# Layer 1's seven products in a ViTDet-like two-layer kernel: w1 in a step of its own, w2 moved between w7 and w4, and the last pair's result one part later

## The chip, the cores and the metric

The kernel runs on one core of a Trainium2 chip, as one program. The metric is device time in microseconds (us). Engines are named as in the profile: PE (TensorE matmul), DVE (VectorE), ACT (ScalarE), POOL (GpSimd) and SP (SyncE, which only issues DMAs here).

## What is computed

Four images of 32 x 32 tokens and 768 channels pass through two residual layers. Each layer is a group norm, an attention with 12 heads of 64 channels and with relative positions by row and column, and an output projection. Layer 1 has in addition a depthwise 3 x 3 convolution and a layer norm on each head's Q, K and V, and adds Q to the attention's result.

```python
x = x + conv0(gn(x))                      # layer 0: plain Q, K, V
x = x + conv1(gn(x))                      # layer 1
# conv1, per image and head:
q, k, v = (layer_norm(dwconv3x3(t, w_pool)) for t in split(x @ w_qkv.T + b_qkv))
attn = q * scale @ k.T + rel_h + rel_w    # rel_* = q with the table of offsets
o = softmax(attn) @ v + q
return o @ w_proj.T + b_proj
```

## The kernel before

**Stages, pairs and items.** A stage is one image's pass through one layer. The order of the eight is (image, layer) = (0,0), (1,0), (0,1), (1,1), (2,0), (3,0), (2,1), (3,1). A stage is six pairs of heads; hp = 0 to 5 is a pair's index in its stage. The 48 pairs are numbered through, and the attention of pair n is called item n here. An item has 16 steps: for each half c of the 512-column query blocks, twice (scores for four key blocks in two steps, product with V in two steps). Layer 1 is in items 12 to 23 and 36 to 47.

**Pieces.** Everything else is cut into pieces hung on steps. `plan` (L833 to L900) lists the pieces of pair i with a step r that counts from the start of item i-1; a negative r lies in item i-2. So during item n the pieces of pair n+1 (r = 0 to 15) and of pair n+2 (r = -16 to -1) run. PE, DVE, ACT, POOL and SP each take their instructions in the order in which the program lists them; an instruction that waits holds all behind it on its engine.

**Seven products.** For a pair of layer 1 whose two predecessors are also in layer 1 (`in_products`, 20 pairs: 14 to 23 and 38 to 47) Q and K of both halves of the tokens, a product of 2 x 2 blocks (token half by channel half, channel half by Q or K), are made by seven products, w1 to w7, instead of eight, with weights (`mix_weights`) and token blocks (`sum_tokens`, the sums S1 to S4) added up in advance. Each product is 12 matmuls. `products(n)` issues them:

- w1, w2 and w6 come first. In 14 of the pairs (hp not 1 or 4) they are at step -7, w1 and w6 summed in one bank; w7 follows at -6 and w4 at -5 in the same bank. In the six early pairs (hp 1 and 4) w1, w6 and w2 are at -8, and w7 and w4, each in a bank of its own, at -6 with two DVE adds (L666, L669).
- w5 at step -4 and w3 at step -2 follow in both; add(w3) (L681) at step 0. `put_from` (L593) is the ACT copy from PSUM to the padded tile.
- DVE then runs the convolution's taps (L706), the layer norm (L721 to L744), ACT the exponentials.

**Other pieces near.** `positions(g)` (L775) is the relative position run on PE, 128 small matmuls a group, two groups a pair, followed by two ACT copies (L780, L781). `split` (L791, L792) splits its result. `back` (L753) transposes the normalised Q and K on PE (tile ln_t). `call` (L605) loads the three token blocks of a sum on SP's queue. `sum_tokens` writes these sums through tile x; `mix_weights` adds up weight sets with five DVE subtractions or additions.

**The result of a pair.** The last row of the pair's attention result is the sum for the softmax. It is turned around by `invert` (a reciprocal on DVE, L950, which waits for a DMA of that row), restored by `restore_last` (PE, L989, tile last) and multiplied by `weighed_result`. These are parts, taken one after another behind scores and products of the next item (L1121 to L1133). The pair with hp = 5 has a list of parts of its own.

Of the kernel before, what the change touches and what calls it, by code (L numbers as in the profile page):

```python
# [17 lines left out]
P = 128  # L18
# [33 lines left out]
def two_layers(ctx: ExitStack, tc: tile.TileContext, keep, x_in, wqkv, wproj, rels, windows, vrow, small, const, onehot, picks, out):  # L52
# [79 lines left out]
    def small_bank(name):  # L132
        return ps_small.tile([P, 512], F32, tag="small", name=name)
# [84 lines left out]
    def in_products(i):  # L218

        return all(items[k][1] == 1 for k in (i, i - 1, i - 2))  # L220

    def shift(i):

        return 4 if i and items[i][1] == 0 and items[i - 1][1] == 1 else 0
# [64 lines left out]
    def used(use):  # L289
        load_weights(uses.index(use) + 2)  # L290
# [53 lines left out]
    def sum_tokens(stage):  # L344


        for n in range(NC // 2):
            x11, x12, x21, x22 = (xns[stage][:, n + k, h : h + HALF] for h in (0, HALF) for k in (0, 3))

            def keep_sum(which, x, y, op):  # L350
                to = wp.tile([P, HALF], F32, tag="x", name="token_sum")
                nc.vector.tensor_tensor(to, x, y, op)
                nc.sync.dma_start(tokens[stages.index(stage) % 2][which, n], to)
                return to

            s1 = keep_sum(S1, x21, x22, ALU.add)
            s2 = keep_sum(S2, s1, x11, ALU.subtract)
            yield
            keep_sum(S4, x12, s2, ALU.subtract)
            yield  # L360
            keep_sum(S3, x11, x21, ALU.subtract)
            yield

    def group_norm(stage):
# [69 lines left out]
    class Pair:  # L434
# [175 lines left out]
            for n in range(3):  # L610
                halves(ps, w[:, n, :], x[n], start=not (n or more), stop=n == 2, skip_group_check=True)

        def second(self):

            self.seven(self.w12, 2, [xns[self.b, self.layer][:, 3 + n, :HALF] for n in range(3)], more=True)
            self.put_from(0, 0, self.w12)

        def products(self, n):

            Q, K = 0, 1
            xn = xns[self.b, self.layer]
            x = {(h, k): [xn[:, 3 * k + n, h * HALF : (h + 1) * HALF] for n in range(3)] for h in range(2) for k in range(2)}
            add = lambda to, x, y: nc.vector.tensor_tensor(to, x, y, ALU.add)  # L627
            early = self.hp in (1, NC // 2 + 1)
            if n == 0:
                temps = one.tile([P, 2, HALF], F32, tag="k0", name="temps")  # L630
                self.u, self.x = temps[:, 0], temps[:, 1]
                self.pad[Q] = in_turn("pad", pads)
                if not early:
                    self.sum, w2 = bank("sum"), bank("w2")
                    self.seven(self.sum, 0, x[0, 0])
                    nc.scalar.copy(self.x, self.sum)
                    self.seven(w2, 2, [xn[:, 3 + m, :HALF] for m in range(3)])
                    self.seven(self.sum, 1, self.blocks, more=True)
                    used((self.i, 0, 0))
                    self.call(S3)  # L640
                    add(w2, w2, self.x)
                    self.put_from(Q, 0, w2)
                    nc.scalar.copy(self.u, self.sum)
                    return
                self.w12, w6 = bank("w1w2"), bank("w6")
                self.seven(self.w12, 0, x[0, 0])
                nc.scalar.copy(self.u, self.w12)
                self.seven(w6, 1, self.blocks)
                used((self.i, 0, 0))
                self.call(S3)  # L650
                self.second()
                add(self.u, self.u, w6)
            elif n == 1 and not early:
                self.seven(self.sum, 3, self.blocks, more=True)
                used((self.i, 0, 1))
                self.call(S1)
                nc.scalar.copy(self.x, self.sum)
            elif n == 5:
                self.seven(self.sum, 4, x[1, 1], more=True)
                self.put_from(Q, 1, self.sum)  # L660
            elif n == 1:
                w7 = bank("w7")
                self.seven(w7, 3, self.blocks)
                used((self.i, 0, 1))
                self.call(S1)
                add(self.x, self.u, w7)  # L666
                w4 = bank("w4", place_b)
                self.seven(w4, 4, x[1, 1])
                add(w4, w4, self.x)  # L669
                self.put_from(Q, 1, w4)  # L670
            elif n == 2:
                self.pad[K] = in_turn("pad", pads)
                w5 = small_bank("w5")
                self.seven(w5, 5, self.blocks)
                used((self.i, 0, 2))
                self.call(S4)
                add(self.u, self.u, w5)
                add(w5, w5, self.x)
                self.put_from(K, 1, w5)
            elif n == 4:  # L680
                add(self.w3, self.w3, self.u)  # L681
                self.put_from(K, 0, self.w3)
            else:
                self.w3 = bank("w3")
                self.seven(self.w3, 6, self.blocks)
                used((self.i, 0, 3))
                after = self.i + 1
                if after < len(items) and in_products(after) and items[after][2]:
                    pairs[after].call(S2)
# [57 lines left out]

        def back(self, s, h):

            ps = bank("ln_t")  # L750
            for t in range(NKT // 2):
                g = h * (NKT // 2) + t
                nc.tensor.transpose(ps[:, t * P : (t + 1) * P], self.c[s][:, g * P : (g + 1) * P], ident)  # L753
            g = LN + 2 * s
            if s == 0:
                self.put_q(ps, h, col(g), col(g + 1))
            else:
                self.put_k(ps, h, sk[:, g : g + 1], sk[:, g + 1 : g + 2])

        def positions(self, g):  # L760


            if g == 0:
                self.whole = one.tile([P, T], F32, tag="whole", name="whole")
            ps = bank("rel")
            for k in range(S // 2):
                at = g * (S // 2) + k
                for j in range(2):
# [36 lines left out]
        def plan(self):  # L805
# [31 lines left out]
            late = self.hp in (0, NC // 2)  # L837
            early_late = self.hp in (1, NC // 2 + 1)
            if in_products(self.i):
                steps = (-8 if early_late else -7, -6, -4, -2, 0)  # L840
                pieces = [(r, lambda n=n: self.products(n)) for n, r in enumerate(steps)]
                if self.hp not in (1, NC // 2 + 1):
                    pieces.append((-5, lambda: self.products(5)))
                if not (self.hp and in_products(self.i - 1)):
                    pieces.insert(0, (-10, lambda: self.call(S2)))
            else:
                pieces = [
                    (-8 if early_late else -7, lambda: self.padded(Q, 0)),
                    (-6, lambda: self.padded(Q, 1)),
                    (-4, lambda: self.padded(K, 0)),  # L850
                    (-2, lambda: self.padded(K, 1)),
                ]
            between = self.i + 1 < len(items) and in_products(self.i + 1) and self.hp + 1 not in (1, NC // 2 + 1)
            positions_1 = lambda: self.positions(1)
            positions_1.last = between
            pieces += [
# [8 lines left out]
                (9, lambda: self.back(Q, 1)),  # L865
                (10, lambda: self.square(K)),
                (11, lambda: self.squares(K)),
                (11 if between else 10, lambda: self.positions(0)),
                (11, positions_1),
                (12, lambda: self.norm(K)),  # L870
                (11 if short(self.i) and self.hp == NC - 1 else 12, lambda: self.split()),
# [39 lines left out]
    def attend(pair, os):  # L911
# [20 lines left out]
        for c in range(T // QC):  # L932
# [152 lines left out]
            for g in range(0, NKT, 4):  # L1085
# [35 lines left out]
                if g + 4 == NKT:  # L1121

                    if not pair.layer:
                        parts = (sums, result, finish) if last(c) else (sums, spread, call, spread_finish)
                    elif not by_ones[c]:
                        parts = (landed, sums, result)
                    elif (pair.hp, c) == (NC - 1, 1):
                        parts = (invert, only_restore, weighed_result)
                    elif short(pair.i) and (pair.hp, c) in ((NC - 2, 1), (NC - 1, 0)):
                        parts = (landed, invert, only_restore, weighed_result)  # L1130
                    else:
                        parts = (landed, invert_and_restore, landed, weighed_result)
                    rest.extend(parts)  # L1133
                    found = copy(av)
# [136 lines left out]
    for k in range(1, len(stages)):  # L1271
# [3 lines left out]
        if stages[k][1]:  # L1275
            places = (34, 37, 41, 41, 50, 50, 53, 55, 57, 59, 61) if stages[k - 1][1] else range(27, 60, 3)
            token_sums = sum_tokens(stages[k])
            for r in (60, *range(64, 72)) if stages[k - 1][1] else range(58, 67):
                at(first + r, lambda token_sums=token_sums: next(token_sums))
        else:  # L1280
            places = (34, 37, 41, 41, 50, 50, 53, 55, 58, 61, 64) if stages[k - 1][1] else range(34, 67, 3)
# [13 lines left out]
    for u, call, step in (  # L1295
        (2, 0, 5), (7, 6, 11), (3, 13, 18), (4, 22, 29), (8, 31, 38), (5, 40, 47), (0, 49, 55), (6, 57, 63), (1, 65, 71),
        (9, 72, 77), (10, 78, 83), (11, 84, 89), (17, 114, 119), (18, 120, 125), (19, 126, 131), (20, 132, 137),
        (15, 212, 217), (14, 226, 233), (16, 258, 265), (12, 266, 274), (13, 275, 281),
    ):
        mix = mix_weights(u)  # L1300
        for at_step in (call, step):
# [361 lines left out]
```

## Time and profile before

| what | value |
|---|---|
| median of 3 runs (lowest to highest) | 3785.4 us (3783.3 to 3787.0) |
| the profiled execution | 3783.47 us |
| its span | 3781.5 us |
| PE busy | 3688.4 us, 98% |
| DVE busy | 2463.0 us, 65% |
| ACT busy | 1724.8 us, 46% |
| POOL busy | 617.4 us, 16% |
| mean granted clock of PE | 0.998 |

The busy shares are averages over the span; the profile's slices show DVE at six to eight tenths in layer 1 and fewer in layer 0. The time of a wait is the idle time of an engine before an instruction, with the event that ended it.

### The profile page before, as it was taken

The page shows a single profiled execution, that of the slowest core. Times are in us where ns is not written, and L with a number is a line of the kernel's source. Part 1 is how long each engine was busy: PE and PEld are TensorE (multiplying, and loading weights), DVE is VectorE, ACT ScalarE, POOL GpSimd, SP SyncE. Part 2 cuts the span into 40 slices and gives each one's busy share as a digit, 9 for nine tenths or more (in the row PEclk, how much of TensorE's full clock was granted, in tenths as well). Part 3 has the DMA queues.
Part 4 walks back from the last instruction along what each step waited for, and adds up shares of the span by engine and source line. Part 5 has one row for each costly group of instructions (what it writes and reads, how often), then busy time and mean ns, then how long its engine had stood idle before and what let it go on. Part 6 is the DMA issues. An engine that isn't in the chain of part 4 may idle for free.

```text
span 3781.5 us, 77865 instructions
## 1 busy us (share of the span) xinstructions
PE 3688.4 (98%) x32926; PEld 1640.7 (43%) x32926; DVE 2463.0 (65%) x3181; ACT 1724.8 (46%) x2438; POOL 617.4 (16%) x1152
## 2 busy tenths in 40 slices
PE   8999999999999999999999999999999999999998
PEld 4535535534344433444535445355343444334442
DVE  2566555559678877688454554445686788767884
ACT  2455434545345553455434544244452555434551
POOL 0111100110121221022310010001101122212130
PEclk9999999999999999999999999999999999999999
DMA  4444454431543564442344232523225435354333
GB/s 149 115 133 125 143 147 130 118 102 49 163 151 106 157 172 117 144 128 81 81 119 132 62 89 69 172 69 107 82 55 167 133 101 165 89 152 118 86 92 103
DMA packets 267347, 441.87 MB, mean 117 GB/s; under 512 B 43446, under 2 KB 115538, under 8 KB 266992
## 3 DMA queue, kind: packets, MB, share of 16 engines
q1 hardware_dynamic: 189008, 321.60, 27.1%
q0 software_dynamic: 77984, 115.21, 13.1%
q8 instruction: 263, 4.31, 0.5%
q14 instruction: 92, 0.75, 0.1%
HBM read 275.38 MB, written 60.39 MB: 89 GB/s over the span
## 4 chain that ended last, share of the span: by engine, by line
PE 82%; DVE 10%; issue 3%; DMA 3%; ACT 1%; POOL 1%; SPq 0%; DVEq 0%; ACTq 0%; POOLq 0%
PE s L1091 15%; PE av L1115 14%; PE qkv L138 9%; PE m1m L138 5%; PE m3m L138 4%; PE m4m L138 4%; PE sum L138 4%; PE s L1093 4%; PE w L138 4%; PE p3p L138 3%; PE p1p L138 3%; PE rel L775 3%; DVE shared L706 2%; PE p4p L138 2%; PE m L138 2%
## 5 line engine op out<-in xcount | busy, mean ns | idle before, releaser
L1098 ACT ACTIVATE e<-s 128x1024 f32<-128x1024 f32 x768 | 767.3, 1023 | 357.7 <-PE s L1093 332.8
L1091 PE MATMUL s<-q,k 64*128 64x512 f32 x3072 | 811.2, 604 | 13.1 <-ACT e L1098 4.7
L706 DVE SCALAR_TENSOR_TENSOR shared<-shared,sm 128x1056 f32<-128x1056 f32 x576 | 757.5, 1315 | 14.9
L1093 PE MATMUL s<-bias,ones 64*128 64x512 f32 x1536 | 613.8, 790 | 0.9 <-DMA bias<-high 0.9
L1115 PE MATMUL av<-e,vt 128*64 128x512 f32 x2624 | 595.9, 596 | 0.1
L802 POOL DMA_DIRECT2D bias<-high x384 | 202.0, 546 | 1774.9 <-ACT high L791 1494.6
L1109 DVE TENSOR_TENSOR acc<-acc,e 128x1024 f32<-128x1024 f32 x294 | 360.2, 1225 | 117.1 <-ACT e L1098 90.9
L1091 PEld LDWEIGHTS s<-q,k 64*128 64x128 f32 x3072 | 279.7, 186 | 276.2 <-issue 195.0
L138 PE MATMUL qkv<-xn,wqkv_t 128*64 128x512 f32 x1728 | 387.3, 598 | 0.9 <-DVE xn L408 0.9
L1115 PEld LDWEIGHTS av<-e,vt 128*64 128x64 f32 x2624 | 184.8, 137 | 347.3 <-issue 300.5
L1093 PEld LDWEIGHTS s<-bias,ones 64*128 64x128 f32 x1536 | 149.8, 187 | 182.9 <-issue 176.2
L138 PEld LDWEIGHTS qkv<-xn,wqkv_t 128*64 128x64 f32 x1728 | 121.1, 138 | 236.5 <-issue 230.7
L802 POOL DMA_DIRECT2D bias<-whole x384 | 206.2, 566 | 43.5 <-DVE whole L792 30.9
L593 ACT ACTIVATE shared<-qkv,sm 128x512 f32<-128x512 f32 (+1 forms) x128 | 57.4, 502 | 284.2 <-PE qkv L138 284.2
L938 ACT COPY weighed<-av 128x512 f32<-128x512 f32 x96 | 56.3, 586 | 246.5 <-PE av L1115 237.3
L1107 DVE TENSOR_TENSOR acc<-e 128x1024 f32<-128x1024 f32 x49 | 60.0, 1224 | 164.0 <-PE z L1013 116.2
L775 PEld LDWEIGHTS rel<-q,rel 64*32 64x32 f32 x6144 | 112.8, 106 | 74.6 <-issue 60.0
L593 ACT ACTIVATE shared<-w,sm 128x512 f32<-128x512 f32 x120 | 53.8, 503 | 196.4 <-DVE w L627 196.4
L956 POOL DMA_DIRECT2D inv<-z_inv x94 | 51.5, 552 | 516.6 <-DVE z_inv L950 428.6
L775 PE MATMUL rel<-q,rel 64*32 64x32 f32 x6144 | 124.3, 195 | 8.5 <-issue 8.5
L721 DVE TENSOR_REDUCE mean<-ln_c 128x8 f32<-128x512 f32 x144 | 98.6, 685 | 48.3 <-PE ln_c L718 48.3
L775 PE MATMUL rel<-q_t,rel 64*32 64x32 f32 x6144 | 125.2, 195 | 4.4 <-issue 4.4
(208 smaller groups left out, 5057.1 us busy)
## 6 DMA issues: line engine op xcount, KB each, us to landing
bias<-high POOLq DMA_DIRECT2D x384, 128.0 KB, 3.3
bias<-whole POOLq DMA_DIRECT2D x384, 128.0 KB, 4.2
blocks<-tokens SPq DMA_DIRECT2D x160, 256.0 KB
wqkv_t<-mixed SPq DMA_DIRECT2D x86, 384.0 KB
wqkv_t<-in_wqkv SPq DMA_DIRECT2D x126, 192.0 KB
third_block<-tokens SPq DMA_DIRECT2D x80, 256.0 KB
wproj_t<-mixed SPq DMA_DIRECT2D x48, 384.0 KB
wqkv_t<-in_wqkv SPq DMA_DIRECT2D x38, 384.0 KB
```

The lines of the kernel that those rows point to most:

```text
L138: nc.tensor.matmul(ps[lo : lo + D], a[:, lo : lo + D], b, start=start, stop=stop, **kw)
L593: nc.scalar.activation(self.pad[s][:, rows, there : there + src.shape[2]], src, AF.Identity, bias=col(self.column(s)))
L706: nc.vector.scalar_tensor_tensor(y, window, tap, y, ALU.mult, ALU.add)
L721: nc.vector.tensor_reduce(of, heads, AX.X, ALU.add)
L775: nc.tensor.matmul(ps[lo : lo + S, k * S : (k + 1) * S].rearrange("p (b c) -> p b c", b=2), rel[rows, 2 * self.layer + i, first : first + ...
L802: nc.gpsimd.dma_start(sets, some.unsqueeze(1).to_broadcast([D // 2, 2, QC]))
L1091: nc.tensor.matmul(ps[:, j, :], k[rows, keys], q[rows, cols], start=True, stop=False)
L1093: nc.tensor.matmul(ps[:, j, :], ones[rows, kt % 2 * P : (kt % 2 + 1) * P], bias[c][rows, kt // 2, :], start=False, stop=True,)
L1098: nc.scalar.activation(e, ps, AF.Exp)
L1107: nc.vector.tensor_tensor(acc, es[0], es[1], ALU.add)
L1109: nc.vector.tensor_tensor(acc, acc, e, ALU.add)
L1115: nc.tensor.matmul(av[j * D : (j + 1) * D, :], pair.vt[:, kt, j * D : (j + 1) * D], e[:, j, :], start=(kt == 0), stop=(kt == NKT - 1),)
```

## The change

In 16 of the 20 pairs (all but hp 2; `in_chain`) w1 stands alone at step -8 with an ACT copy into tile high, w6 is at -7, w7 and w2 are at -6 with one DVE add, and w4 at -5. The first position run of the pair before moves to step 10, ahead of w7 and w2; the second stays at 11. The hp 2 pairs (14, 20, 38, 44) take the form that the early pairs had, with w1, w6 at -7 and w2, w7, w4 at -6. For pairs 17 and 41 (hp 5, with another layer-1 stage behind) the reciprocal and the result come one part later. The token sums S3 are issued last, over the last three calls, and five weight mixes are issued at other steps.

```diff
+    def in_chain(i):
+        return i < len(items) and in_products(i) and items[i][2] != 2
...
-            keep_sum(S3, x11, x21, ALU.subtract)
+        for n in range(NC // 2):
+            xn = xns[stage]
+            to = wp.tile([P, HALF], F32, tag="x", name="token_sum")
+            nc.vector.tensor_tensor(to, xn[:, n, :HALF], xn[:, n, HALF:], ALU.subtract)
+            nc.sync.dma_start(tokens[stages.index(stage) % 2][S3, n], to)
             yield
...
+            if n == 0 and in_chain(self.i):
+                self.w1 = one.tile([P, T], F32R, tag="high", name="w1")[:, :HALF].bitcast(F32)
+                self.sum = bank("sum")
+                self.seven(self.sum, 0, x[0, 0])
+                nc.scalar.copy(self.w1, self.sum)
+            elif n == 6:
+                self.seven(self.sum, 1, self.blocks, more=True)
+                used((self.i, 0, 0))
+                self.call(S3)
+                nc.scalar.copy(self.u, self.sum)
+            elif n == 1 and in_chain(self.i):
+                self.seven(self.sum, 3, self.blocks, more=True)
+                self.call(S1)
+                nc.scalar.copy(self.x, self.sum)
+                w2 = bank("w2", place_b)
+                self.seven(w2, 2, x[0, 1])
+                used((self.i, 0, 1))
+                add(w2, w2, self.w1)
+                self.put_from(Q, 0, w2)
...
-            ps = bank("ln_t")
+            ps = small_bank("ln_t") if s == 0 and h and in_chain(self.i + 1) else bank("ln_t")
...
-            ps = bank("rel")
+            between = in_chain(self.i + 1) and self.layer
+            ps = small_bank("rel") if between and g else bank("rel", place_b) if between else bank("rel")
...
-                steps = (-8 if early_late else -7, -6, -4, -2, 0)
+                steps = (-8, -6, -4, -2, 0, -5, -7) if in_chain(self.i) else (-7, -6, -4, -2, 0)
...
-                    pieces.insert(0, (-10, lambda: self.call(S2)))
+                    pieces.insert(0, (-8, lambda: self.call(S2)))
...
-                (11 if between else 10, lambda: self.positions(0)),
+                (10, lambda: self.positions(0)),
...
-                    elif (pair.hp, c) == (NC - 1, 1):
+                    elif (pair.hp, c) == (NC - 1, 1) and short(pair.i):
                         parts = (invert, only_restore, weighed_result)
                     elif short(pair.i) and (pair.hp, c) in ((NC - 2, 1), (NC - 1, 0)):
                         parts = (landed, invert, only_restore, weighed_result)
                     else:
                         parts = (landed, invert_and_restore, landed, weighed_result)
...
-            for r in (60, *range(64, 72)) if stages[k - 1][1] else range(58, 67):
+            for r in (60, 64, 67, 68, 70, 71, 72, 72, 73) if stages[k - 1][1] else range(62, 71):
...
-        (15, 212, 217), (14, 226, 233), (16, 258, 265), (12, 266, 274), (13, 275, 281),
+        (15, 138, 147), (16, 149, 159), (12, 220, 228), (13, 268, 276), (14, 277, 283),
```

## The prediction

> **What bounds the kernel now.** First the page: the profiled execution took 3783.47 us, 1.97 us of it outside the span, and lies 1.9 us below the median of the runs (3785.4).
>
> ```profile
> span 3781.5 us, 77865 instructions
> PE 3688.4 (98%) x32926; PEld 1640.7 (43%) x32926; DVE 2463.0 (65%) x3181; ACT 1724.8 (46%) x2438; POOL 617.4 (16%) x1152
> ```
>
> PE sets the end: it is idle for 93 us in all. PE's list of instructions keeps its count in this change (the seven products stay seven), so a gain can come only from those 93 us, from time at a lower clock, and from new idle time on the other side. Hence the second view, the waits of PE: us in total, times, longest.
>
> ```profile
> PE rel L775 <- issue: 12.9, 10, 2.2
> PE w L138 <- ACT shared L593: 11.0, 6, 2.2
> PE last L989 <- ACT shared L593: 9.7, 2, 5.0
> PE s L1091 <- ACT e L1098: 4.7, 6, 1.0
> PE sum L138 <- PE ln_t L753: 3.4, 14, 0.2
> PE m3m L138 <- DVE shared L475: 2.7, 3, 1.3
> PE s L1091 <- DVE shared L722: 2.2, 3, 0.8
> PE s L1091 <- ACT whole L781: 1.6, 4, 0.4
> PE sum L138 <- DMA blocks<-tokens: 1.5, 2, 0.8
> ```
>
> The change touches each of these lines. "Item n" is below the attention of pair n, which runs beside pieces for pairs n+1 and n+2. I placed every gap above 0.4 us in its item. Third view: VectorE's timeline in item 20, one of the six items that prepare an index-1 or index-4 pair.
>
> ```profile
> 1668.61 0.70 DVE L627 TENSOR_TENSOR w<-w,temps 128x512 f32<-128x512 f32 x1 [1.95 <-PE w L138]
> 1669.22 1.21 DVE L732 TENSOR_REDUCE lnv<-shared 128x16 f32<-128x1024 f32 x1
> ...
> 1670.55 2.67 DVE L706 SCALAR_TENSOR_TENSOR shared<-shared,sm 128x1056 f32<-128x1056 f32 x2
> 1673.13 0.77 DVE L704 TENSOR_SCALAR shared<-shared,sm 128x1056 f32<-128x1056 f32 x1
> 1673.93 5.45 DVE L706 SCALAR_TENSOR_TENSOR shared<-shared,sm 128x1056 f32<-128x1056 f32 x4
> ...
> 1683.00 0.69 DVE L627 TENSOR_TENSOR w<-w,temps 128x512 f32<-128x512 f32 x1
> ```
>
> Read it as one chain: DVE waits for the product w4, then squares, seven taps, norm, split, and only then the two adds that free w5 for the copies of L593; from the first add's start to those copies' end (1684.69) it is 16.07 us. PE needs only 14.14 us from the end of w4 (1668.51) to the end of the work ahead of product w3 (1682.64), so it stands 2.09 us. The same view in item 18:
>
> ```profile
> 1418.10 0.34 DVE L950 RECIPROCAL z_inv<-z_inv 32x32 f32<-32x32 f32 x1 [6.67 <-DMA z_inv<-z]
> ```
>
> A reciprocal at the head of DVE's queue waits 6.67 us for its DMA, the add of w3 stands behind it, and PE's `last` stands 5.05 us; item 42 is the same with 4.66.
>
> Fourth, the granted clock in windows from the end of a gap (PE busy, instructions, clock, DMA):
>
> ```profile
> 1243.51:1244.51 1.00, 1.00 (x6) 0.50 0.07 16
> 1684.73:1685.73 1.00, 1.00 (x6) 1.00 1.06 221
> ```
>
> After gaps of 2.17, 2.20, 4.66 and 5.05 us the clock is at half for 3.41 us, which loses 1.71 us; after gaps of 2.09 and 2.10 us it stays full.
>
> [...]
>
> **Part 1, w2 behind w7 (16 pairs).** w1 stands alone a step earlier, then ln_t, w6, and after the first position run w7, w2, w4. PE's work is the same. ACT gains four 0.58 us copies, DVE loses four 0.68 us adds; ACT is 46% busy, so nothing. w6 now waits for the copy of w1 out of the same bank; ln_t (1.09 us) covers the copy (0.58 us after 0.1 us); without that cover it costs 0.7 us per pair. ln_t comes forward by two products in the six items: in item 20 its source is ready 36.15 us into the item, w1 ends at 36.40, so it just fits.
>
> - *w3.* DVE's chain now starts at w2, which ends one product (2.68 us with its change-over) earlier against w3: PE has 16.82 us, DVE and ACT need 16.07 plus 0.13 of signalling, margin 0.6. The five stalls of items 14, 20, 38, 41, 44 (2.17+2.09+2.10+2.09+2.10 = 10.55) go, and the half clock behind item 14's 2.17: **12.3**. The other ten pairs, which had no such stall, now have the same margin.
> - *rel.* The two position runs, 128 matmuls each, lie 2.65 us apart in ten items, and in eight of them PE stalls in the middle of the second (2.20, 1.38, 0.49, 1.40, 0.25, 1.41, 0.91, 1.44 = 9.48). Where runs lie at least 3.5 us apart, in 37 other items, there is no stall. They come to lie three products (7.7 us) apart. With the half clock after 2.20: **11.2**. Items 22 and 46 (1.83, 1.61; back to back) are untouched.
> - *Small ones.* The 0.24 us of sum behind ln_t in ten of fourteen places, less 0.4 for changed neighbours: 2.0. s behind `whole` (4 x 0.41): 1.6, as the second run no longer ends the step. **3.6**.
> - *New.* The add to w2 waits for PE and holds the rest of DVE's queue. In items 15 and 39 two normalisations of xn (1.45) and a pair of token sums (1.32) stand between it and w5's adds: 2.77 - 0.6 = 2.15 each, 4.3; that is at the edge between 2.10 and 2.17, so half of 2 x 1.71 is added: **6.0** (bounds 4.3 and 7.7). Item 17: 2.59 for a mix less 0.6 is 2.0, against 1.8 before: 0.2.
>
> **Part 2, the last pair's reciprocal one part later (items 18, 42).** The chain of its DMAs lands while DVE goes on to the add of w3, and `last` is reached some 1.5 us after the copies it waits for. The two waits go (5.05+4.66 = 9.71) with two half clocks (3.42): **13.1**. If the result is then late for its own reader, the next part still lies a whole score-and-product step behind, so I take nothing.
>
> **Part 3, token sums and weight mixes.** The S3 sums come last, some later than before, by one to two steps. Waits of sum for blocks (0.80+0.72) go, since the load is issued earlier: 1.5. s behind L722 in 16 and 40 (0.69+0.72): 1.4, as fewer sums stand ahead of it; 1.4 of the e waits there likewise; 0.6 in item 34. **4.9**. Against it: the third S3 block is written two steps before w7 reads it; in 16 and 40 write plus load (2.1 to 4.6 and 3.1 to 5.1 us in the trace) leaves 0 to 3 us each; I take 0.5, near the short end, as queue neighbours there are short: 1.0. SP's order changes: mixes' loads go ahead of some weight loads and S1 and S2 loads change places with them; no weight load is in the list of waits, so nothing. POOL keeps its list. Item 10 gets a mix's subtractions and sums ahead of the add that m3m waits for (1.29 now): one more us carries it over 2.17, so 1.0+1.71 = 2.7 (bounds 1 and 5).
>
> **Sum.** 12.3+11.2+3.6+13.1+4.9 = 45.1 back; 6.0+0.2+1.0+2.7 = 9.9 lost; net 35.2. 3783.47 - 35.2 = 3748.3; on the scale of the median 1.9 more: 3750.
>
> **Rivals.** *Slower: w3 stalls in all 16 pairs.* For: DVE is 81 to 94% busy in these items, its chain of taps stands behind an add that PE's late product releases, and the margin is 0.6 us where ten pairs had several. Against: in item 20 DVE stood idle 1.95 us before that add, and two adds ahead of it are gone. Once DVE reaches the add 0.6 us late every further us is PE's, times 16; at 2.2 us each the gain is eaten (35), and just there the half clock sets in with 1.71 more: 16 x 3.9 = 62, net +27, 3812. So it decides at 2.8 us of lateness, and just under it there is no change.
>
> *The rel stall is not tied to distance.* The profile names no releaser for it ("issue"), so that it is instructions running out is my reading of where it falls; then 11.2 stays: 3761.4, say 3761. For it: at the same 2.65 us item 37 stalls for 0.25 only and item 13 not at all; against it: none in 37 items with the runs further apart.
>
> [...]
>
> *The moved sums collide.* All bounds at once: 7.7 in 15 and 39, 5 in item 10, 3+1.71 in 16 and 40 each (9.4): 22 instead of 9.7 lost: 3763.
>
> **How the numbers follow.** Forecast (3741 to 3757) 0.55; rel 0.13; collisions 0.14; w3 everywhere 0.12; more gained than I count 0.06. The range 3740 to 3770 takes in the first three and leaves out 0.15 or so. About 0.2%, 7.6 us, is what a measurement can tell from no change: all but the w3 rival are faster by more, 0.88; of its 0.12, 0.03 is no change and 0.09 slower.
>
> **What would show it.** In the profile after: no wait of w for L593 above 0.7 us outside items 15, 17 and 39; `last` gone from the list of waits; rel left with the two of items 22 and 46 (3.4); half clock only where a gap passes 2.1 us. PE busy stays near 3680, idle falls from 93 to some 60. A row "w <- ACT shared" with 10 or more entries would make the prediction wrong, and so would rel stalls at 7.7 us distance.

## The result, and the profile after

The changed kernel takes 3750.0 us (median; 3748.99 to 3754.77) against 3784.35 us for the kernel before in the same comparison. The ratio is 0.9911 with a 95% interval of 0.9894 to 0.9928: faster by 0.9%, or 34 us. The profiled execution of the changed kernel was the slowest of its four, 3754.77 us, 4.8 us above the median; against the profiled execution of before it is 28.7 us shorter.

The page of the changed kernel, span and busy time:

```profile
span 3753.0 us, 77916 instructions
PE 3688.4 (98%) x32926; PEld 1628.6 (43%) x32926; DVE 2457.9 (65%) x3177; ACT 1725.3 (46%) x2442; POOL 617.7 (16%) x1152
```

PE has as many matmuls and the same busy time as before to the tenth of a us. The gain is idle time: span less busy time is 64.6 us, where it was 93.1. The waits of PE (us in total, times, longest), the rows that answer to those of before:

```profile
PE w L138 <- ACT shared L601: 6.5, 3, 2.2
PE s L1096 <- ACT e L1103: 4.5, 6, 1.2
PE rel L782 <- issue: 4.1, 2, 2.2
PE m3m L138 <- DVE shared L483: 3.5, 3, 2.2
PE w L138 <- DMA third_block<-tokens: 2.4, 2, 1.2
```

`last` is gone from this list, and so are sum behind the blocks and s behind `whole`; of sum behind ln_t (3.4 in 14 places) 1.0 in four is left, now before w1. The wait of w for L601 (L593 before) fell from 11.0 to 6.5, that of rel from 12.9 to 4.1, and what is left of rel is items 22 and 46, which the change does not touch (3.4 before). m3m went up, and the wait for the third block is new.

How the time of each item moved tells more than the totals. (Item n starts with the first score product of pair n; us, changed kernel less kernel before, from the two profiled executions.)

| items | change | what it is |
|---|---|---|
| 14, 20, 38, 41, 44 | -4.09, -2.16, -2.18, -2.10, -2.17 | the wait at w3; in 14 also its half clock |
| 18, 42 | -7.37, -7.02 | `last` behind the reciprocal, with its half clock |
| 13, 19, 21, 37, 43 | -1.50, -0.73, -1.47, -0.47, -1.90 | rel (in 13 the wait for the blocks), and the small waits |
| 16, 40 | -3.67, -2.56 | rel, and what stood behind the token sums |
| 15, 39 | +1.38, +3.91 | rel gone (in 15 with its half clock), new waits at w3 and half clock |
| 9, 10, 34 | +1.48, +2.61, -1.43 | m3m behind the moved sums and mixes, in 10 with half clock |
| 22, 46, 47 | +1.15, +0.45, +2.01 | the untouched rel stall, in 22 a wait for ACT, in 47 a half clock |

The chain on VectorE in item 20, which stood in the prediction, now looks like this (start, us, engine, line, operation; in brackets the idle time before it):

```profile
1653.62 0.70 DVE L630 TENSOR_TENSOR w<-w,w 128x512 f32<-128x512 f32 x1 [0.78 <-PE w L138]
1654.22 1.21 DVE L738 TENSOR_REDUCE lnv<-shared 128x16 f32<-128x1024 f32 x1
...
1658.93 5.45 DVE L712 SCALAR_TENSOR_TENSOR shared<-shared,sm 128x1056 f32<-128x1056 f32 x4
...
1668.01 0.69 DVE L630 TENSOR_TENSOR w<-w,temps 128x512 f32<-128x512 f32 x1
```

From the first add's start to the end of the last it is 15.08 us, as before (1668.61 to 1683.69). What moved is PE: w2 is now followed by w4, so PE comes to w3 a product later, and the copies end 0.52 us before the work ahead of w3 does. In 13 of the 16 pairs this room is 0.51 to 0.53 us, and in the other three (items 15, 17 and 39) it is used up.

### The profile page after: what moved, and what is told of

It is laid out like the page before. It is cut to its first block, busy times and chain, and to the rows that moved or that the text cites. A ratio compares the mean times of both kernels' runs of the same rounds, so it can differ in the third digit from the quotient of the medians.

```text
span 3753.0 us, 77916 instructions
## 1 busy us (share of the span) xinstructions
PE 3688.4 (98%) x32926; PEld 1628.6 (43%) x32926; DVE 2457.9 (65%) x3177; ACT 1725.3 (46%) x2442; POOL 617.7 (16%) x1152
## 3 DMA queue, kind: packets, MB, share of 16 engines
q8 instruction: 263, 4.31, 0.5%
## 4 chain that ended last, share of the span: by engine, by line
PE 88%; DVE 6%; DMA 2%; ACT 2%; issue 2%; POOL 0%; SPq 0%; DVEq 0%; ACTq 0%; POOLq 0%
PE av L1120 16%; PE s L1096 16%; PE qkv L138 9%; PE m1m L138 5%; PE sum L138 5%; PE m3m L138 4%; PE m4m L138 4%; PE w L138 4%; PE s L1098 4%; PE p3p L138 3%; PE rel L782 3%; PE p1p L138 3%; PE p4p L138 2%; PE m L138 2%; PE ln_c L724 2%
## 5 line engine op out<-in xcount | busy, mean ns | idle before, releaser
L601 ACT ACTIVATE shared<-qkv,sm 128x512 f32<-128x512 f32 (+1 forms) x128 | 57.5, 503 | 281.8 <-PE qkv L138 281.8
L601 ACT ACTIVATE shared<-w,sm 128x512 f32<-128x512 f32 x120 | 53.7, 503 | 160.7 <-DVE w L630 160.7
L138 PE MATMUL m3m<-xn,wqkv_t 128*64 128x512 f32 x528 | 122.6, 600 | 3.5 <-DVE shared L483 3.5
```

The lines of the kernel that those rows point to most:

```text
L138: nc.tensor.matmul(ps[lo : lo + D], a[:, lo : lo + D], b, start=start, stop=stop, **kw)
L601: nc.scalar.activation(self.pad[s][:, rows, there : there + src.shape[2]], src, AF.Identity, bias=col(self.column(s)))
```

## The experiments

**The reciprocal alone, from both sides.** First the changed kernel without it:

```diff
-                    elif (pair.hp, c) == (NC - 1, 1) and short(pair.i):
+                    elif (pair.hp, c) == (NC - 1, 1):
                         parts = (invert, only_restore, weighed_result)
```

> The changed kernel with the last pair's reciprocal and result where they were before. Theory, that the reciprocal at the head of DVE's queue holds the add of w3 and so PE's tile last: 5.05 + 4.66 of waits and two half clocks of 1.71 come back, 13.1 more, about 3763. Rival, that the rearranged adds of the seven products have taken that wait away by themselves: no change against 3750.

Measured: 3762.97 us, ratio 0.9943 (0.9930 to 0.9957), 13.0 us above the changed kernel. Its list of waits has `last` again, somewhat shorter than in the kernel before (8.3 for two), and each of the two comes with half clock. Then the same line the other way round, in the kernel before:

> The kernel before with one edit: the last pair's reciprocal and result one part later. Theory: the two waits of last (9.7) and their two half clocks (3.4) go, 13.1 less, about 3771, and nothing else moves. Rival, that the later result is late for its own readers: as much comes back at the head of items 18 and 42, 3784.

Measured: 3769.72 us, ratio 0.9967 (0.9955 to 0.9979), 12.5 us below the kernel before in this comparison (3782.18). Items 18 and 42 are 6.9 and 6.5 us shorter in its trace, and no wait of `last` is in its list. The two runs agree: this one line is worth 12.5 to 13 us of the 34, with either order of the products.

**The distance between the position runs.** In the kernel before, only this was changed:

```diff
-                (11 if between else 10, lambda: self.positions(0)),
+                (10, lambda: self.positions(0)),
```

> The kernel before with one edit: the first position run one step earlier, ahead of w7, so that the two runs lie two products (5.2 us) apart and not one (2.65 us) in the items that had one product between. Theory, that the stall goes with distance: 9.5 of stalls and one half clock of 1.7 go, 11 less, about 3773. Rival, that the stall has another cause: the rel waits stay at 9 to 13 us and the time at 3784.

Measured: 3787.25 us, ratio 1.0012 (1.0003 to 1.0021), no gain and, if anything, slower by 0.1%. Its waits of PE show why theory and rival both fell short:

```profile
PE sum L138 <- ACT temps L657: 10.4, 14, 0.7
...
PE rel L775 <- issue: 4.4, 2, 2.4
```

The stall did go with the distance: the runs now lie 6.2 us apart in nine of the ten items and 7.2 in one, none of the ten has it any more, and the two places left are items 22 and 46. But a new wait took its place in 14 items. w4 adds to the bank in which w7 has just ended, and ACT has to copy that bank first (L657). In the kernel before, the position run lay between the two products and hid this copy; with the run moved ahead of w7, nothing hides it:

```profile
1237.49 0.59 ACT L657 COPY temps<-sum 128x512 f32<-128x512 f32 x1 [1.16 <-PE sum L138]
1238.13 1.08 PE L138 MATMUL sum<-xn,wqkv_t 128*64 128x512 f32 x4 [0.74 <-ACT temps L657]
```

So 9.5 us of stall were traded for 10.4 us of waits; two waits for the third block (3.2 us in items 15 and 39) are new as well. In the change it is w2 that fills this place.

**w2 on the other side of w7.** That gives the next experiment, in the changed kernel:

```diff
-                self.seven(self.sum, 3, self.blocks, more=True)
...
                 w2 = bank("w2", place_b)
                 self.seven(w2, 2, x[0, 1])
+                self.seven(self.sum, 3, self.blocks, more=True)
...
```

> The changed kernel with w2 ahead of w7 in the 16 pairs, so that w4 stands right behind w7 again. Theory, that w2 between w7 and w4 is what hides ACT's copy of their common bank (0.74 us of wait in each of 14 items in before_runs_apart): 16 x 0.74 = 12 come back, and w2 itself has to wait for the two copies out of the first run's bank if it shares that bank (1.6 us less 0.5, 16 x 1.1 = 18); against it w3 has a product more of room, which takes away its three waits (6.5) and the half clocks behind them: 3756 to 3774. Rival, that the order of the two makes no difference to PE: 3743 to 3750, from w3's room alone.

Measured: 3758.0 us, ratio 0.9935 (0.9918 to 0.9952), 8 us above the changed kernel. The copy's wait is there in all 16 pairs:

```profile
PE sum L138 <- ACT temps L652: 11.0, 16, 0.7
```

The row of w behind L601 is gone, as expected: in this order the room before w3 is 1.45 to 1.52 us in 14 of the pairs and 0.47 in items 15 and 39. In these two w3 waits for the third block all the same (1.76 and 2.26 us): that wait comes even where VectorE's chain does not hold up w3. Wrong in the expectation was the other term: no wait of w2 for the copies of the first position run is in the trace, since it gets another bank. So w2 between w7 and w4 gives up 1 us of room at w3 and saves 0.69 us of waiting in each pair, a good trade where the room is not used up.

**The runs together.** The opposite of the change, for the stall alone:

```diff
-                (11, positions_1),
+                (10, lambda: self.positions(1)),
```

> The changed kernel with the second position run right behind the first, ahead of w7 and w2. Theory, that the stall goes with the distance between the two runs: each of the 20 items stalls as items 22 and 46 do (1.98 and 2.17 in the changed kernel's profile), some 40 us; w2 ends one run (1.3) later, which is 0.8 over the 0.5 of room before w3, some 13 more; half clocks on top where a gap passes 2.1: 3800 to 3820. Rival, that distance has nothing to do with it: no rel waits but the two there are, only the 13 at w3, about 3763.

Measured: 3831.98 us, ratio 1.0133 (1.0117 to 1.0148), 82 us above the changed kernel and more than expected:

```profile
PE rel L782 <- issue: 44.6, 21, 2.7
PE w L138 <- ACT shared L601: 16.8, 16, 2.2
```

The stall comes back in 17 of the 20 items at 1.8 to 2.7 us each (not in 18, with 0.1 in 16, and in 21 only behind the run, 1.8 us inside the product that follows), and in two others at the edge of the stages; it falls anywhere between the 24th and the 125th matmul of the second run. The expectation's 40 + 13 us of waits are there; too low was its price for the clock: 17 stretches of half clock and one at the end, at a granted clock of 0.992. Half of the time at half clock, the most that it can cost, is 31.2 us, where it is 12.7 in the changed kernel.

**The room before w3.** Four more adds of 128x512 behind the add to w2:

```diff
                 add(w2, w2, self.w1)
+                for _ in range(4):
+                    add(self.w1, self.w1, self.w1)
```

> The changed kernel with four more adds of 128x512 (2.7 us) on DVE right behind the add to w2 in each of the 16 pairs. Theory, that the room before w3 is 0.5 us (from the profile: the copies end 0.51 to 0.53 before the work ahead of w3 does) and every us beyond is PE's: 2.2 us in 13 pairs and 2.7 in the three that have none left, 37 us, and a half clock of 1.7 in some of them, 3787 to 3814: the gain is gone or more. Rival, that DVE catches the time up in its idle stretches: within 5 of 3750.

Measured: 3804.34 us, ratio 1.0059 (1.0044 to 1.0075): slower than the kernel before. The waits of PE, two rows:

```profile
PE w L138 <- ACT shared L601: 33.9, 16, 2.2
...
PE ln_t L761 <- DVE shared L752: 12.6, 16, 3.0
```

The delay shows at two places, since the transposes ahead of w3 wait for the same chain; at w3 itself it is 2.17 or 2.18 us in 15 of the 16 pairs and 1.30 in item 15. Half of the time at half clock is 29.8 us, at a granted clock of 0.992. This is the prediction's slower rival made real: 2.7 us of work at this place turn a gain of 34 us into a loss of 22.

**Token sums and mixes as before.** The third part of the change undone (order and steps of `sum_tokens`, steps of the five mixes):

```diff
-            for r in (60, 64, 67, 68, 70, 71, 72, 72, 73) if stages[k - 1][1] else range(62, 71):
+            for r in (60, *range(64, 72)) if stages[k - 1][1] else range(58, 67):
...
-        (15, 138, 147), (16, 149, 159), (12, 220, 228), (13, 268, 276), (14, 277, 283),
+        (15, 212, 217), (14, 226, 233), (16, 258, 265), (12, 266, 274), (13, 275, 281),
```

> The changed kernel with the token sums and the weight mixes of the kernel before (order and steps). By the prediction's sum this part is worth 4.9 back less 3.7 lost: 1 us, so about 3751: the waits of items 9 and 10 shrink by 1.5 and 2.6, items 15 to 17 and 40 get more sums and mixes ahead of what PE waits for. Rival, that the moved work is what makes room for the new order of the products: new waits at w3 or s in items 14 to 17 and 39 to 41 of 2 us each, 3760 and more.

Measured: 3750.92 us, ratio 0.9920 (0.9906 to 0.9933), not to be told from the changed kernel. In the trace items 9, 10 and 17 are 1.5, 2.1 and 2.1 us shorter than in the changed kernel, items 14, 16 and 34 are 1.2, 1.5 and 1.6 us longer. This part moves waits about and is worth nothing as a whole.

**What stands behind the add to w2 in items 15 and 39.** The changed kernel's waits there are new. PE in item 15:

```profile
1253.91 2.61 PE L138 MATMUL w<-blocks,wqkv_t 128*64 128x512 f32 x8 [2.18 <-ACT shared L601]
1257.71 1.97 PE L138 MATMUL w<-third_block,wqkv_t 128*64 128x512 f32 x4 [1.19 <-DMA third_block<-tokens]
```

VectorE, and SP's own queue, in the same item:

```profile
1235.01 0.70 DVE L630 TENSOR_TENSOR w<-w,w 128x512 f32<-128x512 f32 x1 [4.96 <-PE w L138]
1235.62 1.52 DVE L416 TENSOR_SCALAR xn<-xn,gmean,r_gn 128x1024 f32<-128x1024 f32 x2
...
1247.85 0.69 DVE L356 TENSOR_TENSOR token_sum<-token_sum,xn 128x512 f32<-128x512 f32 x1
```

```profile
1234.93 0.33 SPq L276 DMA_DIRECT2D wqkv_t<-in_wqkv  x1
1247.85 1.05 SPq L357 DMA_DIRECT2D tokens<-token_sum  x2
1249.00 1.82 SPq L613 DMA_DIRECT2D blocks<-tokens  x2
1250.88 0.48 SPq L271 DMA_DIRECT2D wqkv_t<-in_wqkv  x1
1251.41 0.51 SPq L613 DMA_DIRECT2D third_block<-tokens  x1
```

DVE waits 4.96 us for w2, and only behind that add come the normalisation and the sums that were ready to run in this time. The sum's write waits for DVE at the head of SP's queue, and the blocks that w3 needs are loaded behind it. So they were moved to the other side of the add:

```diff
-            places = (34, 37, 41, 41, 50, 50, 53, 55, 57, 59, 61) if ...
+            places = (34, 37, 41, 41, 50, 50, 53, 55, 57, 57, 61) if ...
...
-            for r in (60, 64, 67, 68, 70, 71, 72, 72, 73) if ...
+            for r in (58, 64, 67, 68, 70, 71, 72, 72, 73) if ...
```

> The changed kernel with two normalisations of xn two steps earlier and the first token sum two steps earlier, so that they stand ahead of the add to w2 on DVE and not behind it (items 15 and 39; DVE waits there 4.96 us before that add). Theory, that DVE work behind this add is what delays w3 and that a sum's write holds the next blocks' load on SP's queue: the w3 waits of 2.18 and 2.18, the third-block waits of 1.19 and 1.22 and both half-clock stretches of 6.83 us go, 6.8 + 6.8 = 13.6 less, about 3736. Rival, that VectorE is simply full there: the waits come back elsewhere in items 15, 16, 39, 40 and the time stays within 3 of 3750.

Measured: 3744.07 us, ratio 0.9895 (0.9879 to 0.9910), 5.9 us less than the changed kernel's median, though the two intervals overlap. In the trace items 15 and 39 are 5.4 and 5.8 us shorter and neither wait is left in them; DVE's wait ahead of the add fell from 4.96 to 2.18 us. Items 16 and 40 took 0.6 and 0.7 us back. The time is 8 us above the 3736 expected. The expectation took half of each 6.83 us at half clock as lost, but PE stood idle for 1.2 us of it, which costs nothing more. It also counted the half clock of one profiled execution as if it were in every run; the granted clock of the changed kernel is 0.997 in that execution and 0.998 in its other three.

**A faster version.** With that edit, the last mix one step earlier, and layer 0's mixes and sums in other steps:

> As norm_and_sum_ahead, and besides: the last mix one step earlier (ahead of the add to w2 in item 17), two mixes of layer 0 in other steps of item 9 with their loads behind the result's row on SP's queue, and the layer-0 token sums kept out of the first steps of items 10 and 34. Theory: the w3 wait of item 17 (2.1, at times with a half clock) goes, and the m3m waits of items 9 and 10 (1.1 to 2.0 and 2.2 with a half clock) shrink by 3 to 5: 5 to 8 below norm_and_sum_ahead, about 3738. Rival: SP's queue or the two buffers of tile x make them come back elsewhere, 3744.

Measured: 3739.86 us, ratio 0.9891 (0.9876 to 0.9906). Item 17 is 2.2 us shorter than in the changed kernel, item 9 by 1.4. PE still waits 2.6 us in item 10: a mix and two token sums share the two buffers of tile x and waited for each other's writes. Once more, with these apart (against the changed kernel; the edit of norm_and_sum_ahead is in it too):

```diff
-        (15, 138, 147), (16, 149, 159), (12, 220, 228), (13, 268, 276), (14, 277, 283),
+        (15, 146, 150), (16, 151, 154), (12, 220, 228), (13, 268, 276), (14, 277, 282),
...
-  else range(62, 71):
+  else (60, 61, 62, 66, 67, 68, 69, 70, 71):
```

> As ahead_and_mixes_moved, with the two mixes of layer 0 and its first token sums disentangled: mixes in items 9 at steps 6 and 10, sums from step 12 on, two of them ahead of item 10 no longer in one queue with a mix through the two buffers of tile x. Theory: the m3m wait of item 10 (2.6) shrinks below 1 and nothing else moves, 3738. Rival: the mixes hit item 9's own adds instead, 3740 or more.

Measured: 3737.35 us, ratio 0.9883 (0.9867 to 0.9900), the fastest here: 12.7 us below the changed kernel's median, though the two intervals still overlap a little. The kernel before had medians of 3780.7 to 3784.4 us in the comparisons of these runs, so between two changed kernels a few us are not to be told apart; by the ratios it is 10.6 us, and the last step from 3739.86 is too small to be shown. No wait of w for L601 is left, m3m is down to 1.1 us in three, and no half clock but the one at the end.

## Why the prediction was right, point by point

- *w3, 12.3 forecast.* Right: -2.1 to -2.2 in four items and -4.09 in item 14, 12.7 together. The room was put at 0.6 and is 0.52. The rival of a w3 wait in all pairs did not come, and four_adds_behind_w2 shows where it would have: its price of some 62 us was of the right size (54 measured for 2.7 us).
- *Small ones, 3.6 forecast.* Right: 2.4 us of sum behind ln_t and the 1.6 of s behind `whole` are gone.
- *rel, 11.2 forecast.* Right in the amount (8.8 in the list of waits and the 1.7 of item 15's half clock), and the rival that distance has nothing to do with it is out: no stall in these items at 6.2 and 7.8 us, 44.6 us of it with the runs together. (The runs that lay further apart before were 36, not 37.) The prediction's reading, that PE runs out of instructions there, was not shown: the traces tell when these stalls end, see below, and not what PE waits for. But the prediction gave this gain to the distance alone. before_runs_apart shows that the distance by itself brings nothing, since the run had hidden a copy; the gain hangs on w2 lying between w7 and w4, which the prediction did not see.
- *`last`, 13.1 forecast.* Right: 12.5 and 13.0 by the two experiments.
- *Sums and mixes, 4.9 back and 3.7 lost.* Right as a whole: 0.9 measured for the part by itself, under what can be told. Within it item 10 came as forecast (+2.61 for 2.7). Item 9 was missed: two loads of a mix now stand right ahead of the result's row on SP's queue, DVE's first operation waits 8.41 us for that row and not 7.27, and m3m stands 1.1 us. The row's load is issued as early as before and lands later; that the mix's loads slow it is likely and not shown.
- *New waits in 15 and 39, 6.0 forecast.* Here the step was mis-sized. The wait at w3 is 2.18 for the 2.15 forecast, and in item 17 2.11 for 2.0. Left out was SP: its order had been looked at for the loads of weights ("no weight load is in the list of waits, so nothing"), not for a sum's write that waits for DVE with the blocks' load behind it. That is 1.19 and 1.23 more, and it falls in the 3.41 us at half clock that follow the wait at w3; in both items the stretch at half is 6.83 us long. Less the idle time in it that is some 2.8 lost in each, where 0.86 had been taken. In the profiled execution these two items lose some 12 and not 6.0; norm_and_sum_ahead takes 11.1 off them.
- *The half clock.* "Half clock only where a gap passes 2.1 us" was wrong as a rule, see below: the gap of 2.11 in item 17 has none and the one of 1.99 in item 47 has one. As a coin toss for gaps of that size it was fair: of the seven gaps of 1.98 to 2.21 us in the changed kernel's trace four have one. PE's busy time stayed at 3688.4; the prediction's 3680 is on neither page.

The profiled execution fell 28.7 us and not 35.2. Item by item, more was lost than counted in 15 and 39 (5.1: forecast +0.2 together, measured +5.29), in item 9 (1.5), in item 47 (2.0, half clock behind a gap of 1.99 us that is in the kernel before as well) and in 22 and 46 (1.6), 10.2 in all; some 3.5 of it came back in the other items, spread over many. The median of the four runs lies 4.8 us below this execution, and there the forecast met it. The granted clock is 0.997 in this execution and 0.998 in the other three, so part of that agreement is luck with the clock.

## What to carry to other kernels

Where one engine is busy for 98% of the span, count its idle time gap by gap, and ask of every instruction that is moved what it used to hide: the position run that was too near its twin was also the cover of a copy (0.74 us of wait in each of 14 items without it). Two rows of 128 small matmuls stalled in 8 of 10 places at 2.65 us from each other and in none at 3.5 us and more: put longer ones between two such rows. Before an instruction that waits in an in-order queue put what is ready, behind it what is not: in item 15 DVE stood for 4.96 us before an add, with ready work behind it. That holds for the queue that issues the DMAs as well: in the same item a sum's write waited 12.6 us on SP's queue for DVE, and stopped the loads behind it. A slack of 0.5 us that sixteen places share is a cliff (2.7 us of work in each cost 54 us), and should be measured by loading it.

## What the runs showed of the hardware

**The half clock, in the profiled executions of the two kernels.** Its stretches begin at 1181.23, 1242.67, 1420.16 and 3287.25 us in the kernel before and at 777.17, 1255.04, 3108.47 and 3698.98 us in the changed kernel (the last of each execution, which runs past the end of the work, aside). In each execution every one begins a whole number of 3.413 us after the first, to within 0.01 us, and lasts one or two of these, 3.41 or 6.83 us. Let a window be one such step, with the start-up ahead of item 0 left out. In the window ahead of each of the eight stretches PE was idle for 2.16 to 3.41 us in sum; in every other window at full speed it was idle for 1.74 us or less, and no half clock followed. In the two stretches of 6.83 us PE was idle for 1.19 and 1.20 us of the first window at half; in the other six it was 0.11 us or less.

So gaps of the same size were followed by half clock in one place and not in another. The gap of 2.17 us in item 14 of the kernel before lies inside one window, and half clock follows; the one of 2.17 us in item 46 of the changed kernel has 0.69 us in one window and 1.48 in the next, and none follows. The gap of 2.11 us in item 17 of the changed kernel is divided in the same way (0.57 and 1.54). The gap of 1.99 us near the end (item 47) is divided in the kernel before (1.63 and 0.36), without half clock; in the changed kernel 1.93 us of it and a second gap of 0.24 lie in one window, and half clock follows. An estimate of what a stretch of 3.41 us costs is half of it, 1.7 us at most. The windows of the changed kernel behind the gap of item 15 (PE busy, instructions, clock, DMA):

```profile
1254.00:1255.00 1.00, 1.00 (x6) 1.00 0.94 325
1255.10:1256.10 1.00, 1.00 (x4) 0.50 1.34 361
1260.00:1261.00 1.00, 1.00 (x6) 0.50 1.03 186
1262.00:1263.00 1.00, 1.00 (x10) 1.00 0.99 298
```

The gap ends at 1253.91, and the clock falls only at 1255.04, which is 140 steps of 3.413 us after the first stretch. These are two executions of two kernels; what sets the clock no trace says.

**Two runs of 128 small matmuls near each other.** In the kernel before the second run stalled in 8 of 10 places at 2.65 us from the first (0.25 to 2.20 us) and in both places where the two are back to back (1.83 and 1.61; 1.98 and 2.17 in the changed kernel), and in runs_together in 17 of 20 items, for up to 2.7 us, somewhere inside the run and with no event that ends the wait. At 3.5 us and more there was no stall in 36 places of the kernel before and in 46 of the changed kernel. The waits list names no cause. What the two traces show is when these stalls end. Each page has a queue that it calls instruction (`q8 instruction: 263, 4.31, 0.5%`): 263 packets of 16,384 bytes in both executions, no two of which start less than 3.26 us apart; a position run takes 1.29 us. Of the waits of PE that the profile calls "issue" there are 17 above 0.15 us in the two traces, 12 of them in a position run, and every one ends 1.23 to 1.53 us after such a packet has ended. The stretches from 1.2 to 1.6 us behind the packets are 3% of the span, and of PE's 112 other waits above 0.15 us 6 end in them. That PE runs out of instructions there remains the author's reading: no trace shows what these packets carry or what PE waited for.
